# Layer 2 of a fused convolution stack: the gate as half of one plus tanh, the layer norm's inverse deviation by GpSimd's power

## The chip, the cores and the metric

The kernel runs on one core of one Trainium2 chip. The metric is device time in microseconds, of one whole execution. A core has five engines with instruction streams of their own: TensorE (PE in the profile, its weight loads are PEld), VectorE (DVE), ScalarE (ACT), GpSimd (POOL) and SyncE (SP, which here issues DMAs). [...] ScalarE works its functions out from a table that an instruction of its own, ACT_TABLE_LOAD, puts in place; when the next function isn't in the table that is there, the program has such a load in front of it.

## The reference

Four layers run in sequence on x of 4 images x 64 x 64 positions x 128 channels, float32: a neighbourhood attention (layer 0), a group norm with full attention over the 4096 positions of an image (layer 1), a gated mixing with a layer norm (layer 2), and a two-dimensional selective scan with a depthwise convolution in front (layer 3). The change is in layer 2:

```python
def _layer_norm(x, scale, bias):
    mu = jnp.mean(x, axis=-1, keepdims=True)
    var = jnp.mean(jnp.square(x - mu), axis=-1, keepdims=True)
    return (x - mu) * jax.lax.rsqrt(var + LN_EPS) * scale + bias      # LN_EPS = 1e-05
left = pair @ W_left + b_left
right = pair @ W_right + b_right
gate = jax.nn.sigmoid(pair @ W_gate + b_gate)
left = left + (pair @ W_eq + b_eq)
right_sum = jnp.sum(right, axis=2, keepdims=True)                     # over a row of 64 positions
out = left * right_sum
out = out * gate
out = out @ W_out + b_out
return _layer_norm(out + pair, ln_scale, ln_bias)
```

## The kernel before

An image's activations stay in SBUF as xt, 32 tiles of 128 positions x 128 channels. The four images go through one after the other, and the layers are interleaved: while layer 1 attends over an image, layer 2 and the front of layer 3 work on what is there already. Layer 3's scan and its output come at the end, from about 3060 us on, and the change doesn't touch them.

Layer 1 sets the rhythm. layer_1 runs over 32 blocks i of 128 queries. A block's scores against all 4096 keys come in 8 groups of four key tiles (`score`, L624): PE writes sc into a bank of PSUM, ScalarE copies it to st (L627), VectorE keeps running maxima mx (L630). One step later `fold` (L635) halves mx twice; `turn_maxima` transposes it on PE (pt, L639), VectorE reduces it to nm (L641) and spreads nm on a diagonal, dm (L643); `soften` broadcasts it by a matmul against ones (pb, L647), after which VectorE adds pb to st (L650) and ScalarE takes the Exp (L651). Two steps later `value` (L657) multiplies with v. So in one step of the loop PE works on the scores of block i, the maxima of block i-1 and the values of block i-2. The banks of PSUM for sc, and for the large products of layers 2 and 3, come from one tag with four buffers.

At the end of each step, `between(i)` adds one part of layer 2 and one of layer 3's front. Layer 2 treats the image in 8 chunks of 4 tiles (512 positions); each chunk n goes through four parts, in four steps, and 32 chunks in all (8 x image + n) pass through each part. `n, part = divmod(i - 6, 4)`:

- turn (part 0): four transposes to xT with channels on the partitions, and the row sums rs.
- mix (part 1): pr = right x rs, rt from it on VectorE (L710); pg = gate x xT (L712), sg by ScalarE's sigmoid (L714); pl = left x xT (L716), o1 = (pl + b) * sg on VectorE (L718), o1 times rt on GpSimd (L719), and the output bias added to xt on GpSimd (L723).
- add (part 2): py = o1 x out on PE (L730), xt += py (L732), bn_stats and bn_aggr for each of the four tiles (L736, L737) into mv, which holds mean and variance; then rd, the inverse deviation: ScalarE's root (L739) and VectorE's reciprocal (L740).
- norm (part 3, one step later): x = (x - mean) * rd for each of the four tiles (L747, VectorE, in place), four transposes on PE (pt, L283), scale and bias, and a DMA of the chunk to DRAM for layer 3.

The last chunk's parts come after layer 1's loop, beside layer 0 of the next image (the last image: beside the end of layer 3's front); these are called drains here, and the last one the tail.

Layer 3's front for a chunk: project (pi, L799, copied to xh by ScalarE, L800, and edge rows by GpSimd, L805 and L806), a 3 x 3 depthwise convolution whose taps are shared out (ScalarE multiplies, gsum at L857 and tp at L861; GpSimd adds tp to gsum, L869, and gsum to acc, L872; VectorE takes four taps into acc, L878), gate and activation by Silu (L820), and lower, which multiplies by D (du, L960) and sends rows off.

The order of each engine's instructions is fixed when the program is built, by a scheduler that goes by due times and priorities; only some instructions are pinned to the order written. So instructions that the diff doesn't name can take other places.

Of the kernel before, what the change touches and what calls it, by code (L numbers as in the profile page):

```python
# [22 lines left out]
F32 = mybir.dt.float32  # L23
AF = mybir.ActivationFunctionType
ALU = mybir.AluOpType
# [4 lines left out]
P = 128  # L30
# [51 lines left out]
def conv_seq(ctx, tc, x, mata, matb, cols, rows, rpb, dtw, convw, sel, out):  # L82
# [49 lines left out]

    early = Early()
    layers_0_to_2(tc, xf, mata, matb, rows, rpb, convw, sel, ident, cl, dram, big, ring, early, *fronts)
    layer_3(tc, of, dt, na, ident, cl, big, early, *fronts)


@with_exitstack
def layers_0_to_2(
    ctx, tc, xf, mata, matb, rows, rpb, convw, sel, ident, cl, dram, big, ring, early, x3_d, ub_d, zf_d, y_d, dbl_d, ct_d, gw_d, bw_d  # L140
):
    nc = tc.nc
    wp = ctx.enter_context(tc.tile_pool(name="wa", bufs=1))
# [6 lines left out]
    def ps_s(shape, name):  # L150
        return psp.tile(shape, F32, name=name, tag="s", bufs=4)
# [17 lines left out]
    def m(name, p=P):  # L169
        a, e = MA[name]  # L170
        return ma[0:p, a:e] if e <= nma else once[0:p, a - nma:e - nma]

    def rw(name, tiles=None):
        a, e = ROW[name]
        r = row[:, a:e] if e <= nrow else once[:, NMA - nma + a - nrow:NMA - nma + e - nrow]
        return r if tiles is None else r.unsqueeze(1).to_broadcast([P, tiles, r.shape[-1]])
# [62 lines left out]
    nc.vector.tensor_tensor(w_le, m("left"), m("eq"), ALU.add)  # L239
    b_le = wp.tile([P, 1], F32, name="b_le")  # L240
    nc.vector.tensor_tensor(b_le, cl("b_left"), cl("b_eq"), ALU.add)
    b_rs = wp.tile([P, 1], F32, name="b_rs")
    nc.vector.tensor_scalar(b_rs, cl("b_right"), float(W), None, ALU.mult)

# [34 lines left out]
    def transpose_tiles(src, j0, dst, evac):  # L279

        pt = ps_t([P, 4, P], "pt")
        for k in range(4):
            nc.tensor.transpose(pt[:, k, :], src[:, j0 + k, :], ident)  # L283
        evac(dst, pt.rearrange("p k t -> p (k t)"))
# [12 lines left out]
    def in_blocks(t, n=4):  # L297

        return t.rearrange("p (r b c) -> p r b c", b=n, c=BC)
# [385 lines left out]
    def by_block(t, order):  # L685

        return t.rearrange("p (b r c) -> p " + order, b=4, c=BC)


    eps = wp.tile([P, 1], F32, name="eps2")  # L690
    nc.vector.memset(eps, 1e-5)

    fresh = {}

    def layer_2(b, xt):
        kept = {}

        def turn(n):
            xT = tmp.tile([P, CH], F32, name="x2T", tag="c512", bufs=9)
            transpose_tiles(xt, 4 * n, xT, nc.scalar.copy)  # L700
            rs = sml.tile([P, CH // W], F32, name="rs", tag="rs")
            nc.vector.tensor_reduce(rs, by_block(xT, "r b c"), AX.XY, ALU.add)
            kept[n] = xT, rs

        def mix(n):
            xT, rs = kept.pop(n)
            pr = ps_s([P, CH // W], "pr2")
            nc.tensor.matmul(pr, lhsT=m("right"), rhs=rs, start=True, stop=True)
            rt = sml.tile([P, CH // W], F32, name="rt", tag="rt")
            nc.vector.tensor_scalar(rt, pr, b_rs, None, ALU.add)  # L710
            pg = ps_s([P, CH], "pg2")
            nc.tensor.matmul(pg, lhsT=m("gate"), rhs=xT, start=True, stop=True)  # L712
            sg = tmp.tile([P, CH], F32, name="sg", tag="c512", bufs=9)
            nc.scalar.activation(sg, pg, AF.Sigmoid, bias=cl("b_gate"))  # L714
            pl = ps_s([P, CH], "pl2")
            nc.tensor.matmul(pl, lhsT=w_le, rhs=xT, start=True, stop=True)  # L716
            o1 = tmp.tile([P, CH], F32, name="o1", tag="c512", bufs=9)
            nc.vector.scalar_tensor_tensor(o1, pl, b_le, sg, ALU.add, ALU.mult)  # L718
            nc.gpsimd.tensor_tensor(  # L719
                by_block(o1, "b r c"), by_block(o1, "b r c"), rt.unsqueeze(1).unsqueeze(3).to_broadcast([P, 4, BR, BC]), ALU.mult  # L720
            )
            xs = xt[:, 4 * n:4 * n + 4, :]
            nc.gpsimd.tensor_tensor(xs, xs, rw("b_out", 4), ALU.add)  # L723
            kept[n] = o1

        def add(n):
            o1 = kept.pop(n)
            py = ps_s([P, 4, C], "py2")
            for k in range(4):
                nc.tensor.matmul(py[:, k, :], lhsT=o1[:, bass.ts(k, P)], rhs=m("out"), start=True, stop=True)  # L730
            xs = xt[:, 4 * n:4 * n + 4, :]
            nc.vector.tensor_tensor(xs, py, xs, ALU.add)  # L732
            mv = sml.tile([P, 4, 2], F32, name="mv2", tag="mv2")
            for k in range(4):
                st = sml.tile([P, 6], F32, name="st2", tag="st2")
                nc.vector.bn_stats(st, xt[:, 4 * n + k, :])  # L736
                nc.vector.bn_aggr(mv[:, k, :], st)  # L737
            rd = sml.tile([P, 4], F32, name="rd2", tag="rd2")
            nc.scalar.activation(rd, mv[:, :, 1], AF.Sqrt, bias=eps)  # L739
            nc.vector.reciprocal(rd, rd)  # L740
            kept[n] = mv, rd

        def norm(n):
            mv, rd = kept.pop(n)
            for k in range(4):
                x = xt[:, 4 * n + k, :]
                nc.vector.tensor_scalar(x, x, mv[:, k, 0:1], rd[:, k:k + 1], ALU.subtract, ALU.mult)  # L747
            stays = b == B - 1 and n >= 4
            if stays:
                x3 = fresh[n] = tmp.tile([P, CH], F32, name="x3k", tag="g1")  # L750
            else:
                x3 = tmp.tile([P, CH], F32, name="x3", tag="c512", bufs=9)
            transpose_tiles(
                xt, 4 * n, x3,
                lambda o, i: nc.vector.tensor_scalar(
                    in_blocks(o), by_block(i, "r b c"), cl("ln_s"), cl("ln_b"), ALU.mult, ALU.add
                ),
            )
            if not stays:
                nc.sync.dma_start(x3_d[b][:, bass.ts(n, CH)], x3)  # L760

        return turn, mix, add, norm


# [773 lines left out]
```

## Time and profile before

| | us |
|---|---|
| time, median of 3 runs (lowest, highest) | 3702.48 (3697.66, 3703.27) |
| the profiled execution's span, first to last instruction | 3697.0 |
| the profiled execution's own time | none given beside the span |
| PE busy (TensorE) | 3349.9 |
| DVE busy (VectorE) | 2796.5 |
| ACT busy (ScalarE) | 2699.7 |
| POOL busy (GpSimd) | 1419.4 |
| mean granted TensorE clock | 0.919 |

The span is one execution, and the median of the runs is 5.5 us above it. Times in a row of the profile are microseconds unless marked ns. A row of the timeline gives start, duration, engine, line, operation, output <- inputs, and in brackets how long the engine had been idle and what released it. A row of the waits names the engine and instruction that waited, what for, and how much in all, how often and the longest. A line such as L747 is a line of the kernel; since the diff shifts the lines, the same statement is a few lines further down in the kernel after.

### The profile page before, as it was taken

How to read it: one execution, taken by the hardware profiler on the slowest of the kernel's cores; microseconds unless marked ns; L12 is line 12 of the kernel's file. 1: busy time of each engine (PE TensorE's matmuls, PEld its weight loads, DVE VectorE, ACT ScalarE, POOL GpSimd, SP SyncE). 2: the span in 40 equal slices, each digit the busy share in tenths (PEclk: the TensorE clock that was granted, in tenths of full speed). 3: DMA queues.
4: the chain of work that ended last, by engine and by line, in shares of the span. 5: the costliest groups of instructions: out<-in, count | busy, mean ns of one | idle time of the engine just before them, and what ended most of it. 6: DMA issues, size and time to landing. Idle time of an engine off the chain costs nothing.

```text
span 3697.0 us, 70138 instructions
## 1 busy us (share of the span) xinstructions
PE 3349.9 (91%) x26774; PEld 2768.1 (75%) x26774; DVE 2796.5 (76%) x5227; ACT 2699.7 (73%) x4387; POOL 1419.4 (38%) x1592
## 2 busy tenths in 40 slices
PE   7999999999999999999999999989999997666647
PEld 4789999966899999667999996779999962222236
DVE  4667788866678878666777886767787767999968
ACT  5856677777677777786777777867777778999934
POOL 6500012244122122451222223512221338999866
PEclk8999999999999999999999999999999995555579
DMA  4200000121010012410121212100100269999998
GB/s 132 64 3 30 13 13 30 60 90 34 18 50 27 33 45 79 134 39 15 42 72 33 76 48 94 45 1 24 47 27 33 70 179 240 217 232 211 209 276 281
DMA packets 188308, 310.95 MB, mean 84 GB/s; under 512 B 22303, under 2 KB 110908, under 8 KB 183068
## 3 DMA queue, kind: packets, MB, share of 16 engines
q1 hardware_dynamic: 145316, 220.27, 17.7%
q0 software_dynamic: 24384, 76.95, 11.7%
q10 hardware_dynamic: 18272, 9.24, 0.9%
q8 instruction: 211, 3.46, 0.4%
q14 instruction: 125, 1.02, 0.1%
HBM read 167.69 MB, written 155.56 MB: 87 GB/s over the span
## 4 chain that ended last, share of the span: by engine, by line
PE 59%; issue 13%; DVE 10%; POOL 8%; ACT 7%; DMA 3%; SPq 1%; DVEq 0%; POOLq 0%; ACTq 0%
PE sc L624 17%; PE po L657 17%; PE pt L502 4%; POOL inp L1259 3%; PE sc L467 3%; PE po L513 2%; POOL y L1301 2%; DVE mx L630 2%; DVE acc L878 1%; PE pp L523 1%; PE pz L828 1%; DVE h L1286 1%; PE pb L647 1%; PE pq L595 1%; PE pk L598 1%
## 5 line engine op out<-in xcount | busy, mean ns | idle before, releaser
L624 PE MATMUL sc<-qT,kT 128*128 128x128 f32 x8192 | 1083.9, 276 | 15.8 <-DVE mx L630 15.8
L657 PE MATMUL po<-v,st 128*128 128x129 f32 x8192 | 1080.6, 275 | 2.0 <-ACT st L651 2.0
L624 PEld LDWEIGHTS sc<-qT,kT 128*128 128x128 f32 x8192 | 1000.9, 193 | 38.8 <-issue 26.6
L657 PEld LDWEIGHTS po<-v,st 128*128 128x128 f32 x8192 | 997.9, 192 | 4.7 <-ACT st L651 2.2
L627 ACT COPY st<-sc 128x512 f32<-128x512 f32 x1024 | 574.8, 584 | 426.2 <-PE sc L624 425.5
L630 DVE TENSOR_TENSOR mx<-mx,sc 128x512 f32<-128x512 f32 x768 | 524.0, 682 | 202.3 <-ACT st L627 178.6
L650 DVE TENSOR_TENSOR st<-st,pb 128x2048 f32<-128x2048 f32 x256 | 574.5, 2280 | 4.9 <-PE pb L647 3.8
L651 ACT ACTIVATE st<-st 128x2048 f32<-128x2048 f32 x256 | 483.2, 1908 | 64.7 <-DVE st L650 64.0
L1248 PE MATMUL pdt<-dbl,dt 8*128 8x512 f32 x512 | 307.3, 1079 | 142.1 <-ACT de L1255 141.1
L1259 POOL TENSOR_TENSOR inp<-de,ub 128x1024 f32<-128x1024 f32 x128 | 409.6, 4393 | 9.0 <-DMA y<-du 4.9
L1248 PEld LDWEIGHTS pdt<-dbl,dt 8*128 8x128 f32 x512 | 114.0, 311 | 332.5 <-ACT de L1255 269.5
L493 POOL TENSOR_SCALAR pr<-pr,sm 128x308 f32<-128x308 f32 (+3 forms) x512 | 243.7, 495 | 219.4 <-DVE sm L491 187.3
L723 POOL TENSOR_TENSOR x<-x,row 128x512 f32<-128x512 f32 x32 | 40.8, 1275 | 692.7 <-PE pt L283 692.7
L869 POOL TENSOR_TENSOR gsum<-gsum,tp 128x504 f32<-128x504 f32 (+1 forms) x177 | 240.7, 1363 | 170.9 <-ACT tp L861 84.1
L485 ACT ACTIVATE pr<-pr,mx 128x308 f32<-128x308 f32 (+3 forms) x512 | 262.6, 517 | 0.0
L1286 DVE TENSOR_TENSOR_SCAN h<-h,end,inp 128x1024 f32<-128x1024 f32 x96 | 221.1, 2346 | 18.3 <-ACT h L1272 8.0
L471 DVE CUSTOM_DVE_ANT_0 pr<-sc,bias_m 128x266 f32<-128x266 f32 (+1 forms) x384 | 152.1, 452 | 103.6 <-PE sc L467 103.6
L502 PE MATMUL pt<-ident,pr 128*88 128x128 f32 (+5 forms) x1472 | 203.8, 275 | 8.1 <-ACT prT L504 7.8
L1301 POOL DMA_DIRECT2D y<-yo x112 | 200.7, 2710 | 10.8 <-DVE yo L1300 7.9
L878 DVE SCALAR_TENSOR_TENSOR acc<-xh,cc,acc 128x512 f32<-128x512 f32 (+3 forms) x250 | 199.3, 818 | 4.6 <-ACT acc L842 3.6
L502 PEld LDWEIGHTS pt<-ident,pr 128*88 128x88 f32 (+5 forms) x1472 | 163.5, 138 | 45.6 <-ACT prT L504 31.6
L504 ACT COPY prT<-pt 110x512 f32<-110x512 f32 (+3 forms) x240 | 139.1, 580 | 65.6 <-PE pt L502 65.6
(234 smaller groups left out, 5170.9 us busy)
## 6 DMA issues: line engine op xcount, KB each, us to landing
y<-yo POOLq DMA_DIRECT2D x112, 512.0 KB, 10.6
y<-y SPq DMA_DIRECT2D x48, 512.0 KB
zf_d<-zf SPq DMA_DIRECT2D x64, 256.0 KB
ub_d<-u SPq DMA_DIRECT2D x64, 256.0 KB
ub<-ub_d SPq DMA_DIRECT2D x16, 1024.0 KB
yl<-y SPq DMA_DIRECT2D x64, 256.0 KB
zc<-zf_d SPq DMA_DIRECT2D x64, 256.0 KB
v_d<-vt SPq DMA_DIRECT2D x32, 256.0 KB
```

Of the source, the lines that this page charges most:

```text
L485: pin(nc.scalar.activation(k.pr[:, h], k.pr[:, h], AF.Exp, bias=k.mx[:, h:h + 1], accum_out=k.sm[:, h:h + 1]))
L502: pin(nc.tensor.transpose(pt[0:n, h, :], k.pr[:, h, at:at + n], ident))
L624: nc.tensor.matmul(ps[:, r, :], lhsT=kT[:, bass.ts(G * g + r, P)], rhs=qT[:, bass.ts(i, P)], start=True, stop=True)
L627: nc.scalar.copy(k.st[:, G * g:G * g + G, :], ps)
L630: nc.vector.tensor_tensor(k.mx, k.st[:, 0:G, :] if g == 1 else k.mx, ps, ALU.max)
L650: nc.vector.tensor_tensor(part, part, pb.unsqueeze(1).to_broadcast([P, 16, P]), ALU.add)
L651: nc.scalar.activation(part, part, AF.Exp)
L657: nc.tensor.matmul(k.po, lhsT=k.st[:, j, :], rhs=v[:, j, :], start=(j == 0), stop=(j == NT - 1))
L1248: nc.tensor.matmul(pdt[j][:, g, :], lhsT=dt[o:o + RANK, P * f:P * f + P], rhs=at(dbl[o:o + RANK, :], k & 2, g0, g0 + CH), start=True, stop ...
L1259: nc.gpsimd.tensor_tensor(by_rows(inp), by_rows(de), at(ub_s[f], b ^ (k & 1), SC * n, SC * n + SC), ALU.mult)
L1286: nc.vector.tensor_tensor_scan(h[:, way], h[:, way], inp[:, way], prev, ALU.mult, ALU.add)
L1301: nc.gpsimd.dma_start(here if f == 1 and k == 3 else there, yo, accum_op=ALU.add)
```

## The change

In mix, sigmoid(z) becomes (1 + tanh(z / 2)) / 2: ScalarE takes the Tanh of half the argument (the bias is halved once, at the start), GpSimd adds one in place, and the half goes into rt, as a second operation of the instruction that makes rt. In add, the variance goes to GpSimd, which adds 1e-5 and then raises to the power -0.5, a tile of four columns of -0.5 being the second operand; ScalarE's root and VectorE's reciprocal are gone.

```diff
+    b_gh = wp.tile([P, 1], F32, name="b_gh")
+    nc.vector.tensor_scalar(b_gh, cl("b_gate"), 0.5, None, ALU.mult)
...
-    eps = wp.tile([P, 1], F32, name="eps2")
-    nc.vector.memset(eps, 1e-5)
+    root = wp.tile([P, 4], F32, name="root")
+    nc.vector.memset(root, -0.5)
...
             rt = sml.tile([P, CH // W], F32, name="rt", tag="rt")
-            nc.vector.tensor_scalar(rt, pr, b_rs, None, ALU.add)
+            nc.vector.tensor_scalar(rt, pr, b_rs, 0.5, ALU.add, ALU.mult)
             pg = ps_s([P, CH], "pg2")
             nc.tensor.matmul(pg, lhsT=m("gate"), rhs=xT, start=True, stop=True)
             sg = tmp.tile([P, CH], F32, name="sg", tag="c512", bufs=9)
-            nc.scalar.activation(sg, pg, AF.Sigmoid, bias=cl("b_gate"))
+            nc.scalar.activation(sg, pg, AF.Tanh, bias=b_gh, scale=0.5)
+            nc.gpsimd.tensor_scalar(sg, sg, 1.0, 1.0, ALU.add, ALU.mult)
...
             rd = sml.tile([P, 4], F32, name="rd2", tag="rd2")
-            nc.scalar.activation(rd, mv[:, :, 1], AF.Sqrt, bias=eps)
-            nc.vector.reciprocal(rd, rd)
+            nc.gpsimd.tensor_scalar(rd, mv[:, :, 1], 1e-5, 1.0, ALU.add, ALU.mult)
+            nc.gpsimd.tensor_tensor(rd, rd, root, ALU.pow)
             kept[n] = mv, rd
```

## The prediction

> **What bounds the kernel now.** I read the page's busy shares first, then the waits, the costliest groups of ScalarE, and the timeline around one add.
>
> From the page:
> ```profile
> PE 3349.9 (91%) x26774; PEld 2768.1 (75%) x26774; DVE 2796.5 (76%) x5227; ACT 2699.7 (73%) x4387; POOL 1419.4 (38%) x1592
> ```
> PE sets the time. Up to 3060 us, where everything that the diff touches lies, PE and its weight loads are idle together for only 114 us; in the window 945 to 1510 (layer 1 of image 1) PE is busy for 546.85 of 565.00 us. An edit there counts only through those gaps. ScalarE, which the change relieves, is no bound: it waits for PE's scores (the wait "ACT st L627 <- PE sc L624" is 425.5 us).
>
> The waits that bear on the change (us in total, times, longest):
> ```profile
> PE pb L647 <- DVE dm L643: 23.7, 33, 1.9
> PE sc L624 <- DVE mx L630: 15.8, 9, 3.3
> DVE rd L740 <- ACT rd L739: 31.4, 27, 5.1
> ```
> The first is PE's largest wait in layer 1, about one per add(): PE broadcasts the maxima (pb) once VectorE has made the diagonal dm. The third is VectorE waiting for ScalarE's root, in 27 of 32 adds.
>
> ScalarE's groups (busy, mean ns | idle before):
> ```profile
> L651 ACT ACT_TABLE_LOAD x64 | 82.1, 1283 | 20.8 <-DVE st L650 20.0
> L820 ACT ACT_TABLE_LOAD x37 | 47.5, 1283 | 1.7 <-PE pz L828 1.1
> L714 ACT ACT_TABLE_LOAD x32 | 41.1, 1283 | 2.4 <-PE pg L712 1.3 <-DMA y<-du 0.7
> L739 ACT ACT_TABLE_LOAD x32 | 41.1, 1283 | 0.6
> L739 ACT ACTIVATE rd<-mv,eps 128x4 f32<-128x4 f32 x32 | 9.5, 298 | 7.8 <-DVE mv L737 7.5
> ```
> The sigmoid and the root each need a table load every time, and spoil the table for the Exp and Silu behind them.
>
> The timeline at one add (the ninth of 32, add 8; its last bn_aggr ended at 1086.85; lines of PE, other ACT work and older work left out):
> ```profile
> 1087.74 1.71 POOL L869 TENSOR_TENSOR gsum<-gsum,tp 128x504 f32<-128x504 f32 x1 [0.83 <-ACT gsum L857]
> ...
> 1088.15 1.28 ACT L739 ACT_TABLE_LOAD   x1
> ...
> 1089.78 0.18 DVE L740 RECIPROCAL rd<-rd 128x4 f32<-128x4 f32 x1 [1.45 <-ACT rd L739]
> 1090.00 0.35 DVE L747 TENSOR_SCALAR x<-x,mv,rd 128x128 f32<-128x128 f32 x1
> ...
> 1090.98 1.26 POOL L869 TENSOR_TENSOR gsum<-gsum,tp 128x504 f32<-128x504 f32 x1 [1.53 <-ACT tp L861]
> 1091.05 1.27 DVE L643 TENSOR_SCALAR dm<-ident,nm 128x128 f32<-128x128 f32 x1
> 1092.25 0.85 DVE L747 TENSOR_SCALAR x<-x,mv,rd 128x128 f32<-128x128 f32 x3
> ...
> 1092.47 0.46 PE L647 MATMUL pb<-dm,ones 128*128 128x128 f32 x2 [0.79 <-DVE dm L643]
> ```
> Two things are to be seen. The load makes VectorE wait 1.45 us. And dm, 0.29 us by its median, took 1.27 us: it began 0.07 us after a GpSimd operation and ended with it. That is a rule of this trace: of the dm operations that began inside a GpSimd operation with over 0.3 us left, all 39 ended 81 to 90 ns after it. norm's x (L747), 0.34 us alone, has a median of 1.01 us over the 14 that overlap one. Add 13 shows the same for a chain of GpSimd work:
> ```profile
> 1429.28 5.55 POOL L869 TENSOR_TENSOR gsum<-gsum,tp 128x504 f32<-128x504 f32 x4 [16.74 <-ACT gsum L857]
> ...
> 1430.91 1.15 DVE L635 TENSOR_TENSOR mx<-mx 128x256 f32<-128x256 f32 x1
> ...
> 1432.08 1.64 DVE L878 SCALAR_TENSOR_TENSOR acc<-xh,cc,acc 128x504 f32<-128x504 f32 x1
> 1433.64 1.33 DVE L635 TENSOR_TENSOR mx<-mx 128x128 f32<-128x128 f32 x1
> ```
> While GpSimd runs back to back, each VectorE operation of this kind gets through once per GpSimd operation. I call it the hold.
>
> **The change, part by part.** *Table loads.* The built programs list 300 loads before and 205 after: the 64 of L714 and L739, 29 of the Exp's and 2 of the Silu's are gone. 95 x 1.283 = 121.9 us of ScalarE, and 32 x 0.298 = 9.5 us of roots. On PE's path this is nearly nothing, as ScalarE waits for PE; what it changes is that ScalarE's work inside an add comes earlier.
>
> *Gate.* Tanh replaces Sigmoid, same tile (0.687 us). GpSimd gets a one-input pass over 128x512. No row has this shape: the one-input rows of L493 go from 441 ns (209 wide) to 523 (308 wide), 0.83 ns an element, which extended gives 0.69 us; the ends are 0.52 (the 308 row) and 1.28 (the two-input row of L723, 128x512). I take 0.69. In the mix at 1063 us GpSimd had waited 11.18 us for o1, VectorE's o1 waited 0.50 us for PE's pl anyway, and VectorE was then idle for 4.55 us; nothing on PE waits for o1 until the add, some 18 us later. So in 28 mixes it costs nothing; without that cover it would be 0.7 us each. In the four drains behind layer 1 the gate is on the path ("PE py L730 <- POOL o L719" is 5.9 us, 4 times): the load of 1.28 goes and 0.69 comes. The rt edit only widens one instruction.
>
> *Inverse deviation.* Out: load, root, reciprocal (0.18). In: two 128x4 operations on GpSimd. The add: the smallest one-input rows are 0.15 (memset 128x32) and 0.37 (128x128); I take 0.2. The power p is nowhere in the trace: from 0.15 (that memset) to 1.71 (the longest two-input row above). I take 0.4, near the two-input 128x128 row (L432, 0.455), as it has 1/32 of its elements; that a power is dearer than an add stays for the range.
>
> The cost lies in the order. On GpSimd the built order in ten adds (4, 8, 11, 12, 16, 19, 20, 24, 27, 28) is first gsum, add, power, then gsum, gsum. On VectorE, before: the waiting taps, reciprocal, x, nm, mx, **dm**, x, x, x. After: tap, fold, **x, x, x, x, tap, mx, nm, dm**. So all four x now stand in front of dm. And as ScalarE's tp products are no longer behind a load, both further gsum are ready at once and run back to back over the x. For add 8, from the last bn_aggr: first gsum ends at 2.6; add and power, 3.2; gsum 2 ends at 4.5 and the first x with it; gsum 3 ends at 5.7 and the second x; two free x at 0.28, 6.3; tap 0.73, 7.0; mx 0.68, 7.7; nm 0.2, 7.9; dm inside GpSimd's closing acc (1.27), which the tap released, 8.5. Before it was 5.47, and PE was free at 4.84. So PE's gap grows by about 3.1 us. What is late next is VectorE's st+=pb, and PE's scores that need the bank behind mx: both lie behind the same PE stall.
>
> The sum over adds (number = 8 x image + chunk), each by the same walk:
> - ten as above: 10 x 3.1 = 31.0
> - 10, 18, 26: first gsum ends 1 us earlier (dm 5.27 to 7.5): 3 x 2.2 = 6.6
> - 2 and 3 (dm 4.70 and 4.74 to 7.3 and 6.4): 2.6 + 1.7 = 4.3
> - 29 (dm 4.13, in time, to 8.5, against PE free at 4.84): 3.7
> - 0 and 1, with no gsum to hold them (dm late against 3.80 by four x and a mx): 2 x 1.0 = 2.0
> - 5, 13, 21 (power queued behind four gsum and an acc, one x in front of dm): 3 x 0.5 = 1.5
> - 9, 17, 25: GpSimd idle, rd no later than before: 0
> - drains of images 0 to 2: in the one at 1501 the load (1.28) goes and the pass (0.69) comes, root and reciprocal (0.5) give way to add and power (0.6), level within what p leaves open: 3 x -0.6 = -1.8
> - the last image's tail, where the pass and an acc now stand in front of o1 (1.3 + 0.7, less half a us of loads, taken as 1.3): +1.3
>
> Together +48.6 us: 3697.0 (span) becomes 3745.6. The page gives the profiled execution no other time than its span; the median of the runs is 5.5 above it, so 3702.5 + 48.6 = 3751.1, say 3751.
>
> [...]
>
> **The rivals.** *Faster: rd comes early enough.* The dm gap in the 15 adds 2, 3, 4, 8, 10, 11, 12, 16, 18, 19, 20, 24, 26, 27, 28 sums to 10.9 us, and the load is in that chain. If dm ends by +4.69 in them, 10.9 and the 1.8 of the drains go, less the tail's 1.3: 3691. For it speaks VectorE's wait of 31.4 us for the root. Against it: four x, a tap, mx, nm and dm alone are 4 x 0.28 + 0.73 + 0.68 + 0.2 + 0.28 = 3.0 us, so rd would have to be there at 1.7, before the first gsum is over (2.6). It decides from dm at 4.69. Chance 0.10.
>
> *The hold doesn't stack.* If ScalarE's tp comes as late as before, the x pass between gsums, and dm ends near 5.84 + p = 6.2: +0.8 in 16 adds (the 15 just named and 29), 13, less 0.5 for drains and tail: 3715. Against it: ScalarE loses 1.6 us in front of tp. Chance 0.20.
>
> *The power is slow.* Above 1.71 us it shifts all that follows in the 16 adds of the first four rows: at 2 us 16 x 1.6 = 26 more, 3777; at 3 us 16 x 2.6 = 42 more, 3793. For it: no row shows it. Chance 0.12.
>
> *The change doesn't do what it says*, Tanh loading a table each time: excluded by the built list of 205 loads.
>
> **How the numbers follow.** The forecast (stacked hold) has 0.58. Its own bounds: p from 0.15 (16 x -0.25 = -4) to 1.71 (16 x 1.3 = +21), 3747 to 3772. Towards the others the range runs from 3703, under the middle of the unstacked case, to 3780, just over a power of 2 us; left out are the faster case and a dearer power. About 0.2% (7.4 us) is what a measurement of this kernel can tell from no change. Faster by more: most of the faster case, 0.08. Within: its rest and the low end of the unstacked case, 0.08. Slower: 0.84.
>
> **What would show it.** Right: "PE pb <- DVE dm" grows from 23.7 us to some 70; at add 8 two of the x last over 1 us and dm ends near 8.5; the power's row is 0.4; ScalarE's busy time falls by some 130 us while its wait for PE's scores grows. Wrong: dm in time at add 8; x near 0.34 us throughout; a gap of PE at o1 in the steady mixes; a power row over 2 us.

## The result and the profile after

The changed kernel takes 3817.55 us (median; 3816.58 to 3827.24), the kernel before 3701.84 in the same comparison: the ratio is 1.032, 95% interval 1.0305 to 1.0335. It is slower by some 116 us. The forecast had the sign and the place, at 3751 us, and a range that ended at 3780.

The profiled execution is one of 3827.24 us, with a span of 3825.4. It is 9.7 us above the median, and what is summed over its trace belongs to it. Its busy shares:

```profile
PE 3389.8 (89%) x26774; PEld 2808.2 (73%) x26774; DVE 2864.3 (75%) x5196; ACT 2574.1 (67%) x4260; POOL 1473.7 (39%) x1688
```

ScalarE is relieved of 125.6 us, and has nothing from it. PE, with the same number of instructions, is busy for 39.9 us longer. The waits:

```profile
ACT st L629 <- PE sc L626: 615.6, 495, 9.4
...
PE pb L649 <- DVE dm L645: 120.8, 49, 8.3
...
DVE x L750 <- POOL rd L743: 49.8, 32, 2.9
```

PE's wait for dm has gone from 23.7 to 120.8 us; ScalarE's wait for PE's scores has grown by 190. The loss lies in layer 1's four loops: from the first score matmul of each to its last value matmul they take 2325.9 us together where they took 2188.9, and in them PE is idle for 89.6 us longer and busy for 47.4 longer. All the rest is 8.5 us shorter. GpSimd's new rows and PE's score row (busy, mean ns):

```profile
L743 POOL TENSOR_TENSOR rd<-rd,root 128x4 f32<-128x4 f32 x32 | 33.0, 1033 | 2.3
L717 POOL TENSOR_SCALAR sg<-sg 128x512 f32<-128x512 f32 x32 | 20.2, 631 | 325.5 <-ACT sg L716 325.5
L742 POOL TENSOR_SCALAR rd<-mv 128x4 f32<-128x4 f32 x32 | 7.9, 246 | 73.3 <-DVE mv L740 61.9 <-DVE gate L417 9.9
```
```profile
L626 PE MATMUL sc<-qT,kT 128*128 128x128 f32 x8192 | 1106.0, 280 | 12.6 <-DVE mx L632 12.6
```

The same 8192 score matmuls took 1083.9 us before. Why, is seen further down. First the timeline of GpSimd and VectorE at add 8; its last bn_aggr ended at 1108.98:

```profile
1109.45 1.29 POOL L872 TENSOR_TENSOR gsum<-gsum,tp 128x504 f32<-128x504 f32 x1 [0.83 <-ACT gsum L860]
1110.82 0.20 POOL L742 TENSOR_SCALAR rd<-mv 128x4 f32<-128x4 f32 x1
1111.10 1.02 POOL L743 TENSOR_TENSOR rd<-rd,root 128x4 f32<-128x4 f32 x1
1112.10 2.59 POOL L872 TENSOR_TENSOR gsum<-gsum,tp 128x504 f32<-128x504 f32 x2
1114.77 1.26 POOL L875 TENSOR_TENSOR acc<-acc,gsum 128x512 f32<-128x512 f32 x1
1115.99 2.48 POOL L973 TENSOR_TENSOR u<-u,bb 128x512 f32<-128x512 f32 x2
```
```profile
1112.16 5.17 DVE L750 TENSOR_SCALAR x<-x,mv,rd 128x128 f32<-128x128 f32 x4 [1.28 <-POOL rd L743]
1117.26 1.75 DVE L881 SCALAR_TENSOR_TENSOR acc<-xh,cc,acc 128x504 f32<-128x504 f32 x1
1118.94 0.67 DVE L632 TENSOR_TENSOR mx<-st,sc 128x512 f32<-128x512 f32 x1
1119.53 0.28 DVE L643 TENSOR_REDUCE nm<-pt 128x1 f32<-128x128 f32 x1
1119.85 0.28 DVE L645 TENSOR_SCALAR dm<-ident,nm 128x128 f32<-128x128 f32 x1
```
```profile
1120.28 0.77 PE L649 MATMUL pb<-dm,ones 128*128 128x128 f32 x2 [6.41 <-DVE dm L645]
```

This is the forecast's mechanism. The four x, 0.34 us each alone, take 5.17 us, one for each GpSimd operation of a chain without a pause; the tap behind them is held as well, and dm ends 11.15 us after the last bn_aggr, where it was 5.47. PE waits 6.41 us.

The windows behind that wait hold what the forecast left out (PEclk is the third column from the end):

```profile
1115.00:1120.00 5.00, 0.00 (x0) 0.00 (x0) 4.96 (x6) 0.23 (x1) 3.47 (x3) 0.88 0.42 160
1120.00:1126.00 6.00, 5.72 (x28) 5.75 (x29) 5.05 (x4) 3.00 (x3) 0.00 (x0) 0.53 0.02 4
```

PE comes back to a clock of 0.53, and gets through 28 matmuls in a stretch in which it otherwise does some 55. It is so behind each of the long stalls: over the 6 us that follow, the granted clock is 0.50 to 0.76 behind the sixteen of over 4 us, and 1.00 behind those of 0.58 and 0.85.

### The profile page after: what moved, and what is told of

Read it like the earlier page. It is cut to its first block, busy times and chain, and to the rows that moved or that the text cites. A ratio compares the mean times of both kernels' runs of the same rounds, so it can differ in the third digit from the quotient of the medians.

```text
span 3825.4 us, 69982 instructions
## 1 busy us (share of the span) xinstructions
PE 3389.8 (89%) x26774; PEld 2808.2 (73%) x26774; DVE 2864.3 (75%) x5196; ACT 2574.1 (67%) x4260; POOL 1473.7 (39%) x1688
## 3 DMA queue, kind: packets, MB, share of 16 engines
q14 instruction: 124, 1.02, 0.1%
## 5 line engine op out<-in xcount | busy, mean ns | idle before, releaser
L626 PE MATMUL sc<-qT,kT 128*128 128x128 f32 x8192 | 1106.0, 280 | 12.6 <-DVE mx L632 12.6
L659 PE MATMUL po<-v,st 128*128 128x129 f32 x8192 | 1098.2, 278 | 0.0
L626 PEld LDWEIGHTS sc<-qT,kT 128*128 128x128 f32 x8192 | 1024.6, 196 | 35.5 <-issue 28.9
L659 PEld LDWEIGHTS po<-v,st 128*128 128x128 f32 x8192 | 1015.9, 195 | 3.1 <-issue 2.5
L872 POOL TENSOR_TENSOR gsum<-gsum,tp 128x504 f32<-128x504 f32 (+1 forms) x177 | 231.5, 1310 | 130.8 <-ACT gsum L860 76.4
L632 DVE TENSOR_TENSOR mx<-st,sc 128x512 f32<-128x512 f32 x128 | 87.6, 684 | 196.0 <-ACT st L629 195.9
```

Source lines behind the costliest of these rows:

```text
L626: nc.tensor.matmul(ps[:, r, :], lhsT=kT[:, bass.ts(G * g + r, P)], rhs=qT[:, bass.ts(i, P)], start=True, stop=True)
L632: nc.vector.tensor_tensor(k.mx, k.st[:, 0:G, :] if g == 1 else k.mx, ps, ALU.max)
L659: nc.tensor.matmul(k.po, lhsT=k.st[:, j, :], rhs=v[:, j, :], start=(j == 0), stop=(j == NT - 1))
```

## The experiments

Two runs part the change in its halves. **The gate alone:**

```diff
 (after)
-            nc.gpsimd.tensor_scalar(rd, mv[:, :, 1], 1e-5, 1.0, ALU.add, ALU.mult)
-            nc.gpsimd.tensor_tensor(rd, rd, root, ALU.pow)
+            nc.scalar.activation(rd, mv[:, :, 1], AF.Sqrt, bias=eps)
+            nc.vector.reciprocal(rd, rd)
```

> Only the gate is changed (tanh, GpSimd's pass, the half in rt); root and reciprocal stay as before. Theory A (the loss comes from norm's four x being put in front of dm and held there by GpSimd's chain, then from the lower clock behind the longer PE stalls; both come with the power on GpSimd): built order keeps x behind dm in the steady adds, so 3697 to 3706 us, within 5 us of before, and PE's wait for dm stays near 24 us. Rival C (the gate's pass on GpSimd delays what follows): 32 passes of 0.62 us on the path would give up to 20 us, 3720.

Measured: 3689.63 us (3686.43 to 3693.36) against 3703.0, ratio 0.9964 (0.9952 to 0.9977). Not only does the gate cost nothing, it gains 13 us (0.4%, outside the interval of no change), more than either theory had. In the ten adds in which dm came at 5.47 and late, the built order now has nm, reciprocal and dm in front of the x, and dm comes at 3.9 to 4.2, in time; of the 10.9 us of gaps in the fifteen adds that the rival of a gain had named, 9 are gone. Some of it comes back elsewhere (PE's wait for dm is still 21.8 us in all), and layer 1's four loops, from the first q matmul (pq) to the last value matmul, are 5.8 us shorter together. The three stretches between them, in which the gate's load stood on the path, are 174.5 to 174.9 us each where they were 176.4.

**The power alone** (the kernel before with the two GpSimd operations in place of root and reciprocal):

> Only the inverse deviation is changed (GpSimd's add and power); the sigmoid stays. Theory A: the built order has the four x in front of dm as in the full change, so nearly the whole loss, 3805 to 3825 us, PE's wait for dm near 120 us. Rival C (the gate makes the loss): near 3702.

Measured: 3831.08 us (3828.8 to 3832.82), ratio 1.0346 (1.0331 to 1.036): 128 us slower, and 6 above the range expected. PE's wait for dm is 122.6 us. The halves add up: 128 - 13 = 115. All of the loss belongs to the inverse deviation.

**Which part of it, order or price?** The full change, with norm's four x pinned where the program text has them:

```diff
-                nc.vector.tensor_scalar(x, x, mv[:, k, 0:1], rd[:, k:k + 1], ALU.subtract, ALU.mult)
+                ins = nc.vector.tensor_scalar(x, x, mv[:, k, 0:1], rd[:, k:k + 1], ALU.subtract, ALU.mult)
+                tc.keep_in_program_order(ins)
```

> The full change, with norm's four x pinned to the place that the program text gives them, behind the step's dm and the adds of pb. GpSimd's work is the same, the power included. Theory A: dm waits for a tap or two and a fold, and comes at 4.4 to 5.5 us after the last bn_aggr as before (PE free at 4.84), so the time goes back to 3685 to 3705 us and the clock behind the adds stays 1.00. Rival B (the power's own time, 1.02 us in place of a root, is what costs, wherever x stands): 32 x 1.2 = 38 us at least stay, 3740 or more.

Measured: 3698.0 us (3696.08 to 3702.9), ratio 0.9988 (0.9979 to 0.9997). With every GpSimd operation still there, the whole loss is gone; dm comes at 4.77 in add 8, against PE free at 4.89. But the x of the last two chunks now stand late in the tail: from the end of layer 1 to layer 3's first matmul it is 63.2 us, where the gate alone has 54.7. The same without the pin there (`if b < B - 1 or n < 6:`):

> The full change with norm's x pinned behind the step's work as in the run that stood at 3698, but not for the last two chunks of the last image, where the pin made the stretch between layer 1 and layer 3 8 us longer. Expected 3686 to 3694 us, level with the gate alone (3689.6): with the order mended the power on GpSimd costs nothing, and gains nothing over the root. Rival (the power has a cost of its own): stays at 3697 or above.

Measured: 3688.53 us (3685.63 to 3695.52), ratio 0.9968 (0.9956 to 0.9981), the tail 51.4 us. PE's wait:

```profile
PE pb L649 <- DVE dm L645: 20.7, 31, 1.9
```

GpSimd's chain is still closed up at add 8, whose last bn_aggr ended at 1083.42, and dm is held once and ends 4.77 us after it:

```profile
1086.85 2.60 POOL L874 TENSOR_TENSOR gsum<-gsum,tp 128x504 f32<-128x504 f32 x2
1089.52 1.27 POOL L877 TENSOR_TENSOR acc<-acc,gsum 128x512 f32<-128x512 f32 x1
```
```profile
1087.10 1.09 DVE L645 TENSOR_SCALAR dm<-ident,nm 128x128 f32<-128x128 f32 x1
```

So the mended change is 14 us (0.3%) under the kernel before, as far as the gate alone is: in the right order no cost of the power is to be seen, and no gain over the root.

**The power's price.** The power is left out: a product of the same tiles takes its place, and the built order of all engines is the same.

```diff
-            nc.gpsimd.tensor_tensor(rd, rd, root, ALU.pow)
+            nc.gpsimd.tensor_tensor(rd, rd, root, ALU.mult)
```

> The full change with the power replaced by a product of the same two tiles (rd is then not the inverse deviation: the power is left out). The built order of all five engines is that of the full change. Theory A: the power row falls from 1.02 to 0.2 us or so, rd comes 0.8 us earlier, but the four x stand in front of dm and are held as before: 16 adds x 0.8 = 13 us less, 3798 to 3810. Rival B (the power's own time makes the loss): back to 3740 or less.

Measured: 3802.18 us (3799.97 to 3805.37), ratio 1.0274 (1.0258 to 1.029). The row falls as expected:

```profile
L743 POOL TENSOR_TENSOR rd<-rd,root x32: 197/202/443, 342.5 to 3126.6; 128x4 f32<-128x4 f32 x32
```

The 0.8 us at each add come back as 15 us, and 100 stay. The power is dear, five times a product of its shape (1.02 us against 0.20), but its price is some 13% of the loss.

**Is it the order alone?** The reverse: the kernel before, its root and reciprocal kept, with the x put in front of nm and dm:

```diff
 (before: the loop over the four x moved from norm to the end of add, and)
+            with tc.issue_after(last_x[0]) if k.behind else ExitStack():
+                nc.vector.tensor_reduce(nm, pt, AX.X, ALU.max, negate=True)
```

> The kernel before (sigmoid, root and reciprocal), with norm's four x put in front of nm and dm in the steps behind an add, as the change orders them. ScalarE's loads still stand in front of tp, so GpSimd's order and its pauses between the gsum are those of before. Theory A: rd is there at 3.1 us as with the power, but the x find GpSimd idle for the most part: dm ends at 6 to 7.5, PE's gaps are 1 to 2.5 us, 3715 to 3755 us. Rival O (the order alone is the whole loss, whatever GpSimd does): 3800 or more. Rival N (the order costs nothing): within 5 us of before.

Measured: 3696.55 us (3695.21 to 3701.21), ratio 0.9988 (0.9979 to 0.9997). My theory expected a loss of 12 us at least; the rival that the order costs nothing came nearest (it said within 5 us of before; the time is 6 us less). VectorE and GpSimd at add 8 (last bn_aggr at 1092.79):

```profile
1095.72 0.18 DVE L744 RECIPROCAL rd<-rd 128x4 f32<-128x4 f32 x1 [1.45 <-ACT rd L743]
1095.94 1.12 DVE L747 TENSOR_SCALAR x<-x,mv,rd 128x128 f32<-128x128 f32 x4
1096.97 0.68 DVE L632 TENSOR_TENSOR mx<-st,sc 128x512 f32<-128x512 f32 x1
...
1097.88 0.39 DVE L646 TENSOR_SCALAR dm<-ident,nm 128x128 f32<-128x128 f32 x1
```
```profile
1093.68 1.71 POOL L872 TENSOR_TENSOR gsum<-gsum,tp 128x504 f32<-128x504 f32 x1 [0.83 <-ACT gsum L860]
1096.92 1.27 POOL L872 TENSOR_TENSOR gsum<-gsum,tp 128x504 f32<-128x504 f32 x1 [1.52 <-ACT tp L864]
```

The first x begins 3.15 us after the last bn_aggr, and in the full change 3.18: with the root, rd is there no later. But GpSimd waits 1.52 us for tp, which is behind ScalarE's load, and the four x slip through that pause in 1.12 us. dm ends at 5.48, as before.

Add 2 of the same run has the other case, still with the sigmoid, the root and the reciprocal. There GpSimd's last three passes follow each other without a pause, the four x in front of dm take 4.23 us, and PE waits 3.80 us, where it waited 0.95 in the kernel before:

```profile
481.82 2.92 POOL L872 TENSOR_TENSOR gsum<-gsum,tp 128x504 f32<-128x504 f32 x2 [1.64 <-ACT tp L864]
484.82 1.26 POOL L875 TENSOR_TENSOR acc<-acc,gsum 128x512 f32<-128x512 f32 x1
```
```profile
482.20 4.23 DVE L747 TENSOR_SCALAR x<-x,mv,rd 128x128 f32<-128x128 f32 x4
```
```profile
488.07 0.49 PE L650 MATMUL pb<-dm,ones 128*128 128x128 f32 x2 [3.80 <-DVE dm L646]
```

With the mended run this makes four corners. Where GpSimd pauses: x behind dm 3702 (before), in front 3697. Where its chain is closed up: x behind 3689, in front 3818. Neither the order nor the chain costs anything alone (the corners with the pause have the sigmoid, which is worth 13 us, not 120). At add 8 the pause stands in the three traces that keep the root (1.53 us before, 3.30 with the gate alone, 1.52 here) and in none with the power on GpSimd, be it with sigmoid or with tanh: it goes with the root and its table load. That the load alone holds it open is read from the timeline; no run has the load without the root.

**The hold, tried from the x's side.** The full change, with the sum left in PSUM, so that x reads its tile there:

```diff
-            nc.vector.tensor_tensor(xs, py, xs, ALU.add)
+            nc.vector.tensor_tensor(py, py, xs, ALU.add)
 (bn_stats reads py[:, k, :], and)
-                nc.vector.tensor_scalar(x, x, mv[:, k, 0:1], rd[:, k:k + 1], ALU.subtract, ALU.mult)
+                nc.vector.tensor_scalar(x, py[:, k, :], mv[:, k, 0:1], rd[:, k:k + 1], ALU.subtract, ALU.mult)
```

> The full change, with o + x left in the bank of PSUM that holds py: bn_stats and norm's x read it there, and x writes xt. So x has one input, in PSUM. The built order changes a little: two or three x in front of dm in place of four. Theory A, as the hold is told by the trace (operations whose inputs are all in SBUF are held, reads of PSUM such as nm are not): each x takes 0.3 to 0.4 us although GpSimd runs its chain beside it; dm alone is still held once, ending near 6 to 7 us, so PE's gaps are 1 to 2 us, no lower clock behind them, and the time is 3705 to 3730 us. Rival H (an x beside GpSimd is slow whatever it reads, for instance through contention on the output): x stays at 1.3 us and the time above 3770.

Measured: 3761.86 us (3760.08 to 3775.09), ratio 1.0167 (1.015 to 1.0183). Minimum, median and maximum of x (ns), here and in the full change:

```profile
L750 DVE TENSOR_SCALAR x<-py,mv,rd x128: 397/402/411, 345.8 to 3090.8; 128x128 f32<-128x128 f32 x128
```
```profile
L750 DVE TENSOR_SCALAR x<-x,mv,rd x128: 331/508/1424, 348.6 to 3154.8; 128x128 f32<-128x128 f32 x128
```

Not one of the 128 is held, so rival H falls. The time is over my 3730 for three reasons that the trace shows: at add 8 the work in front of the first gsum lies otherwise, so that it starts at 1.82 instead of 0.47, rd comes at 4.48 and dm at 7.12; eight of the fourteen stalls of 2.1 to 2.5 us that this leaves, which I had taken for safe, are followed by a clock of 0.72; and in adds 12 and 28 dm is held for 5.9 us beside GpSimd's DMA issues, which makes stalls of 7.5 us with a clock of 0.58 and 0.50 behind them. PE's wait for dm is 71.8 us.

**The clock.** The full change, with work added for PE to do while it waits:

```diff
 (soften, in the 16 steps with a stall of over 4 us)
+                for j in range(30):
+                    ins = nc.tensor.matmul(pb, lhsT=ones, rhs=ident, start=True, stop=True)
```

> The full change, with 30 matmuls more (some 4 us, their result is overwritten) put in front of pb in the 16 adds where PE waits over 4 us for dm: 480 matmuls added, nothing taken away, other engines' order all but the same. If the granted clock falls because PE stands idle (theory A's second term, PE's busy time up by 40 us), the clock behind these adds goes back to 1.00 in most of them and the time falls by 20 to 35 us, to 3783 to 3800, although work was added. Rival K (the lower clock is no cost of its own, or comes from something else than PE's idling): 3815 or more.

Measured: 3797.55 us (3793.25 to 3805.56), ratio 1.0262 (1.0248 to 1.0276): 20 us less than the full change, with 480 matmuls more. The window behind the same add, and the score row:

```profile
1118.00:1124.00 6.00, 6.00 (x56) 6.00 (x55) 4.64 (x6) 5.16 (x5) 0.00 (x0) 1.00 0.01 3
```
```profile
L628 PE MATMUL sc<-qT,kT 128*128 128x128 f32 x8192 | 1084.4, 276 | 13.1 <-DVE mx L634 13.1
```

dm comes no earlier (11.18 at add 8), but the clock stays at 1.00 and the score matmuls are back to 1084.4 us. The added matmuls take some 6.7 us, not 4, so that they themselves hold pb up behind dm, by about 16 us in all (0.1 us at add 8, 2.4 at the worst). Add 17, which got none, lost its stall of 3.3 us as well. So by this run the lower clock is worth about 20 + 16 - 3 = 33 us, and PE's busy time had grown by 39.9. That K was wrong is shown; 33 to 40 us is an estimate from these two sums.

## Why the prediction was right in place and sign, and wrong in size

The place, the sign and the mechanism of the forecast hold: the x in front of dm, the closed-up chain, the hold. The rival of a gain fell, by its own condition (dm at 4.69 or earlier): dm ends at 11.15. That the hold doesn't stack fell with the 5.17 us of the four x, and the slow power with 1.02 us against 1.71. The loss is 116 us where 49 were forecast. Two steps failed: the walk of an add behind its second x, which made the stalls too short, and the price of a stall, which had no term for the clock. By their own numbers:

- *The walk of add 8* gave dm at 8.5; it was 11.15, so the stall grew by 5.6 us and not by 3.1. Up to rd the walk was right by accident: the first gsum ended at 1.76 and not 2.6 (it began 0.42 us earlier and took 1.29 us, not 1.71), and the power took 1.02 and not 0.4, so rd came at 3.14 (walk: 3.2). The failed step is "two free x" and the free tap. I had the closing acc wait for the tap behind the x, and GpSimd idle meanwhile. It does not: acc runs right behind the gsum, at 1114.77, and then two products of layer 3's front (u, L973), so the last two x and the tap are held as well (8.36 and 10.03 in place of 6.3 and 7.0). A chain that closes up pulls in all that queues behind it, and I had looked only at its named members.
- *The same in other adds.* Of the sixteen named ones, the stalls are 4.1 to 8.3 us. The three longest, adds 12, 16 and 18, have GpSimd's own DMA issues among the chain.
- *The clock* is the term that the sum lacked: 33 to 40 us. The profile before had the row to see it: its longest stall in layer 1, 3.25 us, is followed by

```profile
966.30:972.30 6.00, 5.91 (x38) 5.94 (x39) 4.24 (x7) 4.59 (x6) 0.68 (x1) 0.72 0.01 3
```

Stalls that grow past that length had to be charged with it.

- *The gate* was put at -0.5 us (drains -1.8, tail +1.3) and its pass at 0.69; the pass is 0.63, and the gate alone is worth -13. The stretches with the drains give 1.5 to 1.9 us each, and the loops 5.8 together, where dm was built in front of the x: gaps that I had put into the rival of a gain.
- *The power* at 0.4 was 1.02, within the bounds; at 16 adds that error is 10 us by my sum; the run without the power agrees with such a sum (0.8 us, 16 adds, 13 us expected and 15 measured).
- *Table loads*: 95 fewer, none on PE's path, as argued. ScalarE's busy time fell by 125.6 us, of which 121.9 are the loads at the trace's 1283 ns.
- *One reading* of the profile before was wrong, and the sum doesn't rest on it. The rule of the hold, given as all of 39, holds beside passes with two inputs (42 of 42 dm ended 81 to 90 ns after the pass); one dm beside a pass with one input (dg, at 2539.49) and one that began in a DMA issue (at 1982.24) took 0.44 and 0.27 us.

On the hold: with its tile read from PSUM x took 0.40 to 0.41 us in all 128, beside the 1.15 to 1.42 of the 62 held ones in the full change. There nm, which reads PSUM, took 0.27 to 0.29 us in all 128, and mx, with sc from PSUM, 0.67 to 0.69 in all 896. By what GpSimd holds the others, no row shows. On the clock: of the stalls of over a microsecond that stand alone in nine of these traces (by the windows of 6 us behind them), 44 of 46 of up to 1.8 us have a clock of 1.00, 17 of the 37 of 1.8 to 2.6 us a lower one, and so do all 49 of 3.2 us and more; but two of 3.3 us in the tails (of the mended run and of the run with x from PSUM) still have 1.00. So in these runs a lower clock came now and then behind a stall of under 1.8 us already, and behind one of 3.3 us it was not yet certain.

## What to carry to other kernels

Before counting a freed engine as a gain, ask what its waits had kept apart: here a pause on GpSimd, behind a load on ScalarE, let VectorE's path work through, and the half of the change that closed it lost 128 us, as four x had come in front of that work. When a build is free to reorder, read the order that it made, and if short work that nobody waits for has come in front of the operation that the bounding engine waits for, pin it back: one line took the loss away. Charge a long stall of the matmul engine with its length and with the slower clock behind it: here 17 of the 37 stalls of 1.8 to 2.6 us that stand alone had one, and all 49 of 3.2 us and more outside the tails; it came to some 2 us more for each (an estimate: 33 to 40 us over 20 stalls).

## What the runs showed of the hardware that was not expected

- A power on GpSimd over 128x4 takes 1.02 us, a product of the same tiles 0.20.
- The product u stands on both engines in one shape (before, L970, 128x512): the median is 1.29 us on GpSimd and 0.68 on VectorE, there with its second input in PSUM.
- The hold lasted through more than one operation where GpSimd issued DMAs. At add 17 of the full change dm began inside a DMA issue and took 3.68 us, through the issues and both passes behind them, where beside back-to-back passes alone a held x took 1.3 to 1.4 in most cases:

```profile
1974.86 3.68 DVE L645 TENSOR_SCALAR dm<-ident,nm 128x128 f32<-128x128 f32 x1
```
```profile
1974.09 1.84 POOL L965 DMA_DIRECT2D y<-du  x2 [0.84 <-ACT du L963]
1975.29 3.15 POOL L973 TENSOR_TENSOR u<-u,bb 128x512 f32<-128x512 f32 x2
```

  In the run with x from PSUM two dm took 5.91 and 5.94 us in the same way (adds 12 and 28). In the kernel before, the dm that began 0.07 us into a DMA issue was not held at all (0.27 us). Why dm did not end at a boundary there stays open.
- Matmuls that nobody needs, put into the stalls, made the changed kernel 20 us faster.
